# Context rows turned in 32x32 blocks and moved by way of DRAM in an attention kernel on one core, with the fourth block's period reordered

## The chip, the core and the metric

The kernel runs on one NeuronCore of a Trainium2 chip. The core's engines run side by side, each through its own list of instructions in order: TensorE (PE) multiplies matrices and loads weights (PEld), VectorE (DVE), ScalarE (ACT) and GpSimd (POOL) do elementwise work, reductions and 32x32 transposes, and SyncE (SP) issues most of the transfers. Engines wait for each other through semaphores. The metric is the time of one execution on the device in microseconds (us). A time below is the median of several runs.

## What is computed

Cross attention with adaptive layer norm, all in float32, for 16 batches of 1024 query rows and 64 context rows of 512 features, 16 heads of 32 features:

```python
def _ada_ln(x, c, W_ss, b_ss):
    h = (x - mean(x)) / sqrt(var(x) + EPS)
    scale, bias = split(silu(c) @ W_ss + b_ss, 2)
    return (1.0 + scale)[:, None, :] * h + bias[:, None, :]

xq  = _ada_ln(x_q,  t_vec, Wss_q,  bss_q)
xkv = _ada_ln(x_kv, t_vec, Wss_kv, bss_kv)
q    = xq @ Wq + bq
k, v = split(xkv @ Wkv + bkv, 2)              # per head
attn = softmax(q @ k.T / sqrt(32))            # per head
out  = x_q + (attn @ v) @ Wp + bp
```

The change concerns `xkv`: the normalised context rows have to be turned, features onto partitions, and get a scale and a bias for each feature and batch, before TensorE makes keys and values from them.

## The kernel before

The 16 x 1024 query rows are cut into 32 blocks of 512 rows, `i` = 0 to 31, two blocks to a batch. The schedule is written out by hand: a helper call issues its instructions at once onto the engines that it uses, so the order of calls is the order of each engine's queue. Blocks 0 to 3 have their periods written out line by line (the fourth block's period, `i` = 3, begins with `scores(3, 0)` at L1154 and ends with `q_scale(7)` at L1221). Blocks 4 to 29 run through one loop (L1224 to L1315), and a tail follows.

A period of the loop is a pipeline over several blocks. It makes the scores of block `i` in two halves (`scores`, L674: 32x32 matmuls into two pairs of PSUM banks of the pool `ps_s`, which has two buffers), their maxima (DVE, L698), a copy to SBUF (ACT, L707), the subtraction of the spread maxima (POOL, L742) and the exponential (ACT, L748). Beside this it mixes the values of block `a = i - 1` (`mix`, L839, L855), divides (`divided`, L835), and projects blocks `a` and `b = i - 2` as seven products each on half-size operands (`product`, L970, added to the residual by DVE at L994). It makes the queries of block `n = i + 1`, again as seven products (`query_product`, L633). Products 1, 6, 5 and 3 of the queries add up in one PSUM bank and 2, 7 and 4 in another; `query_added` (DVE, L670) reads the bank after product 5 and `query_out` (ACT, L663) after 2, 6, 7 and 3, and product 3 goes on in the bank that product 5 left, so it waits until `query_added(n, 5)` has read it.

Query rows of later blocks are prepared in the same periods: statistics (`q_stats`, DVE, L263 and L264; then `q_scale`), normalisation (`hidden`, ACT, L324), a 32x32 block transpose (`turn`, DVE, L503, into the tile `ht`), and sixteen transfers of 64 KB that carry the blocks to their partitions (`move`, L516, into `xt`). The pool of `ht` has **one buffer**. For blocks 1, 2, 3 and 5 half of the sixteen transfers are issued by POOL, all others by SP. `scale_features` (ACT, L573) and `feature_sums` (POOL, L608 to L611) then work on `xt`. The sums of the softmax (`row_total`, DVE, L791) are inverted and carried by way of a small DRAM tile (`inverse_rows`, L809 and L811: one store, four loads), and `spread_rows` (DVE, L817) spreads them.

Context rows come in pairs of batches: 128 rows, so one context tile serves four blocks. In the loop a pair `kvb` passes through four periods, by `kv = i % 4`: load and statistics (0); normalisation (`context_hidden`), four transposes on PE against an identity matrix into PSUM (`context_turned`, L351), scale on DVE (`context_scale`, L369) and shift on POOL (`context_shift`, L373) (1); keys (`key_products` on PE, L398, `key_tiles` on DVE, L409) (2); values (`value_products` on PE, L434, `value_tiles` on DVE, L447) (3). The PSUM results of these helpers lie in a `spare` buffer of `ps_s` (L345), the pool that the scores use. Pair 0 is made in the prologue. Pair 2 gets its features in the third block's period and its keys and values in the fourth (L1202, L1208, L1214, L1215).

Of the kernel before, what the change touches and what calls it, by code (L numbers as in the profile page):

```python
# [9 lines left out]
F32 = mybir.dt.float32  # L10
AF = mybir.ActivationFunctionType
ALU = mybir.AluOpType
# [3 lines left out]
P = 128  # L16
# [4 lines left out]
def cross_attention_block(  # L21
# [51 lines left out]
    nc = tc.nc  # L73

    B, LQ, H = x.shape
    LKV = context.shape[1]
# [69 lines left out]
    def load_residual(i):  # L146

        tag = "r" if i < NB - 1 else "x"
        r = xpool.tile([P, NT, H], F32, tag=tag, name=f"r_{i}")
        nc.sync.dma_start(r, rows_of(x, i))  # L150
        r_tiles[i] = r
# [13 lines left out]
    at = 0  # L165
# [133 lines left out]
    def q_stats(i, ts=range(NT), kvb=None):  # L299

        if ts[0] == 0:
            q_mv[i] = small.tile([P, NT + 1, 2], F32, tag="mvq", name=f"mvq_{i}")
        for t in ts:
            row_stats(q_mv[i][:, t, :], x_tiles[i][:, t, :])
        if kvb is not None:
            row_stats(q_mv[i][:, NT, :], ctx_tiles[kvb])
# [21 lines left out]
    def hidden(i, ts):  # L328

        for t in ts:  # L330
            normalise(x_tiles[i][:, t, :], x_tiles[i][:, t, :], q_rstd[i], t)
# [8 lines left out]
    def context_hidden(b):  # L340
        hk = kvpool.tile([P, H], F32, tag="hk", name=f"hk_{b}")
        normalise(hk, ctx_tiles.pop(b), *kv_rstd.pop(b))
        hk_tiles[b] = hk

    def spare(name):  # L345
        return ps_s.tile([P, 2, TB], F32, tag="s", name=name)[:, 0, :]

    def context_turned(b, pt):
        hk = hk_tiles.pop(b)
        for c in range(NC):  # L350
            nc.tensor.transpose(pt[:, c * P : (c + 1) * P], hk[:, c * P : (c + 1) * P], ident)  # L351
        xk_tiles[b] = kvpool.tile([P, NC, P], F32, tag="xk", name=f"xk_{b}")

    pkt_tiles = {}

    def context_scaled(b):
        pkt_tiles[b] = spare(f"pkt_{b}")
        context_turned(b, pkt_tiles[b])

    def by_batch(t):  # L360
        return t.rearrange("p c (j k) -> p c j k", j=2)

    def of_batches(b, at):
        t = ss["kv"][:, at : at + NC, b : b + 2]
        return t.unsqueeze(3).to_broadcast([P, NC, 2, LKV])

    def context_scale(b):
        pt = pkt_tiles.pop(b).rearrange("p (c k) -> p c k", c=NC)
        nc.vector.tensor_tensor(by_batch(xk_tiles[b]), by_batch(pt), of_batches(b, 0), ALU.mult)  # L369

    def context_shift(b):
        xk = by_batch(xk_tiles[b])
        nc.gpsimd.tensor_tensor(xk, xk, of_batches(b, NC), ALU.add)  # L373

    def context_features(b):
        pt = bank(f"pkt_{b}")
# [29 lines left out]
    def key_tiles(b):  # L406
        pk = pk_tiles.pop(b)
        kt = kvpool.tile([P, NC, P], F32, tag="kt", name=f"kt_{b}", bufs=2)
        nc.vector.tensor_tensor(  # L409
            kt,  # L410
            pk.rearrange("p (c k) -> p c k", c=NC),
            bk_t.unsqueeze(2).to_broadcast([P, NC, P]),
            ALU.add,
        )
        for j in range(2):
            k_tiles[b + j] = kt[:, :, j * LKV : (j + 1) * LKV]
# [153 lines left out]
    def scale_features(i, cs=range(NC)):  # L570
        xt, b = xt_tiles[i], i // BPB
        for c in cs:
            nc.scalar.activation(  # L573
                xt[:, :, c, :],
                xt[:, :, c, :],
                AF.Identity,
                scale=ss["q"][:, c, b : b + 1],
                bias=ss["q"][:, NC + c, b : b + 1],
            )
# [35 lines left out]
    def query_product(i, n):  # L615

        w, t = sums_of["wq"], sums_of["xt"]
        a, x = {
            1: (query_half(0, 0), feature_half(i, 0, 0)),
            2: (query_half(0, 1), feature_half(i, 1, 0)),  # L620
            3: (w[:, 3], feature_half(i, 1, 1)),
            4: (query_half(1, 1), t[:, 2]),
            5: (w[:, 0], feature_half(i, 0, 1)),
            6: (w[:, 1], t[:, 1]),
            7: (w[:, 2], t[:, 0]),
        }[n]
        k = 0 if n in (1, 6, 5, 3) else 1
        new = n in (1, 7)
        if new:
            qa[k] = bank(f"pq_{i}_{n}", k)  # L630
        for m in range(2):
            for c in range(HC):
                nc.tensor.matmul(  # L633
                    qa[k][:, m * HT : (m + 1) * HT].rearrange("p (g n) -> p g n", g=2),
                    lhsT=a[:, c, m * P : (m + 1) * P],
                    rhs=x[:, :, c, :],
                    start=new and m == 0 and c == 0,
                    stop=c == HC - 1,
                    skip_group_check=True,
                )  # L640
# [24 lines left out]
    def query_added(i, n):  # L665

        k, h = {5: (0, 1), 4: (1, 0)}[n]
        for o in (2, 3):
            src, dst = query_places(i, h, k, o)
            nc.vector.tensor_tensor(dst, src, dst, ALU.add)  # L670
# [118 lines left out]
    def row_total(i):  # L789
        lt_tiles[i] = small.tile([P, HPC, NJ], F32, tag="lt", name=f"lt_{i}")  # L790
        nc.vector.tensor_reduce(  # L791
            lt_tiles[i],
            sum_tiles.pop(i).rearrange("p r (j a) -> p r j a", a=32),
            AX.X,
            ALU.add,
            apply_transpose=True,
        )
# [393 lines left out]
    added(2, 1)  # L1191
    product(2, 2)
    added(2, 2)
    load_residual(3)
    q_stats(7)
    weights(3, 1)
    total(3)
    query_product(4, 7)
# [2 lines left out]
    row_sums(2, 1)  # L1201
    key_products(2, spare("pk_2"))  # L1202
    hidden(6, range(NT))
    query_product(4, 5)
    query_added(4, 5)
    row_total(3)
    inverse_rows(3)
    key_tiles(2)  # L1208
    query_product(4, 4)
    query_added(4, 4)  # L1210
    scale_features(5)
    turn(6, range(NT))
    load_x(8)
    value_products(2, spare("pv_2"))  # L1214
    value_tiles(2)  # L1215
    query_product(4, 3)
    query_out(4, 3)
    feature_sums(5)
    product(2, 7)
    move(6)  # L1220
    q_scale(7)  # L1221


    for i in range(4, NB - 2):  # L1224
        a, b, n, f = i - 1, i - 2, i + 1, i + 2
        kvb = i // 4 * 2 + 2
        kv = i % 4 if kvb < B else None
        if kv == 0:
            load_context(kvb)
        scores(i, 0, crossed=True)  # L1230
        product(b, 6)
        added(b, 6)
        query_product(n, 1)
        query_seed(n)
        added(b, 7)
        scores(i, 1)
        product(b, 5)
        added(b, 5)
        maxima(i)
        subtract(i)  # L1240
        product(b, 4)
        if i + 3 < NB:
            hidden(i + 3, (0, 1, 2))
        query_product(n, 2)
        query_out(n, 2)
        product(b, 3)
        spread_rows(a)
        if i + 3 < NB:
            hidden(i + 3, (3,))
        added(b, 4)  # L1250
        added(b, 3)
        biased(a, 2)
        load_residual(i)
        mix(a)
        divided(a)
        row_sums(a, 0)
        query_product(n, 6)
        weights(i, 0)
        query_out(n, 6)
        if kv == 1:  # L1260
            context_hidden(kvb)
        scale_features(f, (0, 1))
        product(a, 1)
        if i + 4 < NB:
            q_stats(i + 4, (0,))
        added(a, 1)
        product(a, 2)
        if i + 4 < NB:
            q_stats(i + 4, (1,))
        added(a, 2)  # L1270
        weights(i, 1)
        total(i)
        query_product(n, 7)
        query_out(n, 7)
        biased(a, 3)
        scale_features(f, (2, 3))
        row_sums(a, 1)
        if kv == 1:
            context_scaled(kvb)
        if kv == 2:  # L1280
            key_products(kvb, spare(f"pk_{kvb}"))
        if kv == 3:
            value_products(kvb, spare(f"pv_{kvb}"))
        if i + 3 < NB:
            turn(i + 3, range(NT))
        if i + 5 < NB:
            load_x(i + 5)
        elif i == NB - 3:
            load_residual(NB - 1)
        query_product(n, 5)  # L1290
        query_added(n, 5)
        if i + 4 < NB:
            q_stats(i + 4, (2,))
        if kv == 1:
            context_scale(kvb)
        if kv == 2:
            key_tiles(kvb)
        if kv == 3:
            value_tiles(kvb)
        query_product(n, 4)  # L1300
        query_added(n, 4)
        if i + 4 < NB:
            q_stats(i + 4, (3,), kvb=kvb if kv == 0 else None)
        query_product(n, 3)
        query_out(n, 3)
        feature_sums(f)
        product(a, 7)
        row_total(i)
        inverse_rows(i)
        if i + 3 < NB:  # L1310
            move(i + 3)
        if i + 4 < NB:
            q_scale(i + 4, kvb=kvb if kv == 0 else None)
        if kv == 1:
            context_shift(kvb)  # L1315

# [135 lines left out]
```

## Time and profile before

| What | Value |
|---|---|
| Median of 3 runs | 1044.82 us (1042.91 to 1045.44) |
| The profiled execution's own time | 1045.25 us |
| Its span, first to last instruction | 1043.3 us |
| DVE / ACT / POOL busy | 82% / 59% / 75% |
| Key products (L398), 256 matmuls in all | 29.9 us |
| Value products (L434), 1024 matmuls in all | 29.6 us |
| Context transposes on PE (L351), 32 matmuls | 4.8 us |
| Context scale on DVE (L369), 6 instructions | 3.9 us |
| Context shift on POOL (L373), 6 instructions | 6.3 us |

The page of a profile lists the busy time of the engines, the chain of work that ended last (followed back from the last instruction, each step to what released it), and groups of instructions with their time and the idle time ahead of them. The trace answers further questions: a timeline of one engine (start, length, line, shapes, and in brackets the idle time ahead with what ended it), sums by window, and landings of transfers. Matmuls overlap and their ends are modelled, so the time that a stretch of matmuls takes is read from start to start.

### The profile page before, as it was taken

The numbers are of one execution on the slowest core, as the hardware profiler recorded it, in microseconds if no ns is written. First come the engines' busy times: TensorE is split into PE (matmuls) and PEld (weight loads), VectorE is DVE, ScalarE is ACT, GpSimd is POOL, SyncE is SP. The second block draws the span as 40 slices with busy tenths as digits, with TensorE's granted clock in tenths as the row PEclk, the third lists the DMA queues.
The fourth block names the chain that finished last, engine by engine and source line by source line (L and its number), as shares of the span: only waits on it lengthen the run. The fifth ranks groups of instructions, "written<-read, shape, count | busy, mean of one in ns | idle before, by whom it ended". The sixth has DMA issues, their size and how long they took to land.

```text
span 1043.3 us, 22968 instructions
## 1 busy us (share of the span) xinstructions
PE 1021.9 (98%) x9058; PEld 760.0 (73%) x9058; DVE 854.4 (82%) x1159; ACT 610.9 (59%) x945; POOL 781.5 (75%) x502
## 2 busy tenths in 40 slices
PE   5999999999999999999999999999999999999998
PEld 3635686778777777777777787778787778777746
DVE  5798977987788977987878878898778997776795
ACT  3666755665567655766556666567557665565530
POOL 0479795887868868888668986688876886977861
PEclk9999999999999999999999999999999999999999
DMA  9851555444454434554335454344354444335122
GB/s 341 250 162 54 150 180 154 128 136 139 154 156 143 125 117 140 166 164 132 117 112 161 154 159 133 110 139 155 137 163 118 141 141 131 102 123 161 45 87 84
DMA packets 103499, 147.63 MB, mean 142 GB/s; under 512 B 33464, under 2 KB 34640, under 8 KB 103392
## 3 DMA queue, kind: packets, MB, share of 16 engines
q1 hardware_dynamic: 102368, 144.08, 43.5%
q0 software_dynamic: 1024, 2.10, 0.9%
q8 instruction: 71, 1.16, 0.5%
q14 instruction: 36, 0.29, 0.1%
HBM read 79.02 MB, written 34.60 MB: 109 GB/s over the span
## 4 chain that ended last, share of the span: by engine, by line
PE 91%; DVE 5%; DMA 1%; ACT 1%; POOL 1%; issue 1%; SPq 0%; DVEq 0%; ACTq 0%; POOLq 0%
PE pp L970 35%; PE pq L633 33%; PE po L855 6%; PE ps L681 6%; PE pq L546 4%; PE pv L434 3%; PE pk L398 3%; DVE m L698 1%; DMA x<-in_x_dram 1%; DVE bs L263 1%; DVE ht L503 0%; POOL s L742 0%; DVE lt L791 0%; ACT s L748 0%; DVE l L753 0%
## 5 line engine op out<-in xcount | busy, mean ns | idle before, releaser
L742 POOL TENSOR_TENSOR s<-s,mb 128x2048 f32<-128x2048 f32 x62 | 281.3, 4564 | 171.3 <-DVE mb L729 167.2
L707 ACT COPY s<-ps 128x1024 f32<-128x1024 f32 x128 | 129.4, 1012 | 112.7 <-DVE m L698 69.5
L698 DVE TRANSPOSE_TENSOR_REDUCE m<-ps 128x32 f32<-128x1024 f32 x128 | 150.8, 1215 | 31.1 <-PE ps L681 29.5
L970 PE MATMUL pp<-w_p_sb,ot 128*128 128x256 f32 x744 | 171.0, 379 | 0.9 <-DVE ot L835 0.5
L994 DVE TENSOR_TENSOR r<-pp,r 128x512 f32<-128x512 f32 x210 | 136.3, 670 | 32.1 <-PE pp L970 25.0
L663 ACT ACTIVATE qt<-pq,bias_t 128x256 f32<-128x256 f32 x224 | 92.6, 464 | 116.0 <-PE pq L633 113.3
L970 PEld LDWEIGHTS pp<-w_p_sb,ot 128*128 128x128 f32 x744 | 141.0, 190 | 21.8 <-issue 1.7
L748 ACT ACTIVATE s<-s 128x2048 f32<-128x2048 f32 x64 | 122.3, 1911 | 41.8 <-POOL s L742 40.0
L786 POOL TENSOR_TENSOR sum<-s,s 128x2048 f32<-128x2048 f32 x30 | 136.2, 4541 | 5.5 <-ACT s L748 5.5
L970 PEld LDWEIGHTS pp<-WT,s 128*128 128x128 f32 x496 | 90.6, 191 | 57.0 <-issue 35.2
L970 PE MATMUL pp<-WT,s 128*128 128x256 f32 x496 | 124.2, 394 | 0.2 <-POOL s L949 0.2
L970 PE MATMUL pp<-WT,ot 128*128 128x256 f32 x496 | 117.6, 380 | 1.0 <-POOL ot L946 0.6
L633 PE MATMUL pq<-xt_sums,wq_sums 128*128 128x256 f32 x448 | 108.5, 385 | 0.0
L633 PEld LDWEIGHTS pq<-xt_sums,wq_sums 128*128 128x128 f32 x448 | 82.9, 190 | 32.8 <-issue 21.8
L633 PE MATMUL pq<-xt,wq_sums 128*128 128x256 f32 x448 | 106.6, 381 | 0.0
L633 PE MATMUL pq<-xt,w_q_sb 128*128 128x256 f32 x448 | 106.0, 379 | 0.3 <-ACT pq L645 0.3
L970 PEld LDWEIGHTS pp<-WT,ot 128*128 128x128 f32 x496 | 93.9, 190 | 16.6 <-POOL ot L946 2.3
L324 ACT ACTIVATE x<-x,rstdq 128x512 f32<-128x512 f32 x128 | 96.6, 807 | 1.9 <-DVE rstdq L294 1.9
L670 DVE TENSOR_TENSOR qt<-pq,qt 128x256 f32<-128x256 f32 x112 | 42.0, 417 | 66.5 <-PE pq L633 66.1
L633 PEld LDWEIGHTS pq<-xt,w_q_sb 128*128 128x128 f32 x448 | 85.0, 190 | 13.1 <-ACT xt L573 0.8
L263 DVE BATCH_NORM_STATS2 bs<-x 128x6 f32<-128x512 f32 x128 | 86.9, 679 | 7.3 <-DMA x<-in_x_dram 7.3
L633 PEld LDWEIGHTS pq<-xt,wq_sums 128*128 128x128 f32 x448 | 83.5, 190 | 11.9 <-issue 1.4
(128 smaller groups left out, 1583.4 us busy)
## 6 DMA issues: line engine op xcount, KB each, us to landing
x<-in_x_dram SPq DMA_DIRECT2D x32, 1024.0 KB, 5.9
r<-in_x_dram SPq DMA_DIRECT2D x32, 1024.0 KB, 5.5
out_dram<-r SPq DMA_DIRECT2D x60, 512.0 KB, 3.7
xt<-ht SPq DMA_DIRECT2D x464, 64.0 KB, 2.0
wss_q<-in_L_xcond_Wss_q_dram SPq DMA_DIRECT2D x2, 1024.0 KB, 9.1
ctx<-in_ctx_dram SPq DMA_DIRECT2D x8, 256.0 KB, 3.1
wss_kv<-in_L_xcond_Wss_kv_dram SPq DMA_DIRECT2D x2, 1024.0 KB
w_kv_sb<-in_L_xcond_Wkv_dram SPq DMA_DIRECT2D x1, 2048.0 KB
```

What stands on the lines that cost most here:

```text
L263: nc.vector.bn_stats(bs, r)
L324: nc.scalar.activation(dst, src, AF.Identity, bias=rstd[:, 1, j : j + 1], scale=rstd[:, 0, j : j + 1])
L633: nc.tensor.matmul(qa[k][:, m * HT : (m + 1) * HT].rearrange("p (g n) -> p g n", g=2), lhsT=a[:, c, m * P : (m + 1) * P], rhs=x[:, :, c, : ...
L663: nc.scalar.activation(dst, src, AF.Identity, bias=bq_t[:, o : o + 1])
L681: nc.tensor.matmul(pss[r // 2][32 * c : 32 * c + 32, r % 2, :], lhsT=kt[rows, c, z * HK : (z + 1) * HK], rhs=qt[rows, c, :], start=True, s ...
L698: nc.vector.tensor_reduce(m_tiles[i][:, z, 2 * e : 2 * e + 2, :], pss[e].rearrange("p r (j a) -> p r j a", a=32), AX.X, ALU.max, apply_tra ...
L707: nc.scalar.copy(s_sb[:, 2 * e : 2 * e + 2, :], pss[e])
L742: eng.tensor_tensor(s_tiles[i, z], s_tiles[i, z], mb_tiles[i], ALU.subtract)
L748: nc.scalar.activation(p, p, AF.Exp, scale=SCALE)
L786: nc.gpsimd.tensor_tensor(t, s_tiles[i, 0], s_tiles[i, 1], ALU.add)
L970: nc.tensor.matmul(acc[k][:, t * HO : (t + 1) * HO], lhsT=rows[:, c, t * P : (t + 1) * P], rhs=cols[:, c, :], start=n == 2 and t == 0 and ...
L994: nc.vector.tensor_add(r, a, r)
```

## The change

The context rows no longer go over TensorE to be turned. `context_turn` transposes them on DVE in 32x32 blocks, `context_move` stores the result to a DRAM tile with one transfer and reads it back with four, and `context_moved` scales and shifts with eight ScalarE instructions of 128x64 elements. This holds for pairs 4 to 14; pairs 0 and 2 keep their way over PE. In the loop the turn and the move stand in the second of the four periods, the scaling in the third, the keys in the fourth, and the values in the first period of the blocks that use them (`i % 4 == 0`, pair `i // 2`). So pair 2's values leave the fourth block's period for the fifth's. The fourth block's period is reordered: `turn(6)` and `move(6)` go ahead of `key_tiles(2)`, `q_stats(7)` is spread out and ends in block 4's period together with `q_scale(7)`, `scale_features(5)` is cut in two, and `row_total(3)`, `inverse_rows(3)`, `load_x(8)` and `load_residual(3)` go behind `query_out(4, 3)`.

```diff
+    def context_turn(b):
+        t = kvpool.tile([P, 4, NC, 32], F32, tag="ctx", name=f"ctx_turned_{b}")
+        nc.vector.transpose(
+            t.rearrange("p k c n -> p c k n"),
+            hk_tiles.pop(b).rearrange("p (c k n) -> p c k n", c=NC, k=4),
+        )
+        turned_tiles[b] = t
+
+    def context_move(b):
+        d = dram.tile([4, 32, 4, NC * 32], F32, tag="ctx", name=f"ctxd_{b}")
+        m = kvpool.tile([P, 4, NC, 32], F32, tag="hk", name=f"ctx_moved_{b}")
+        nc.sync.dma_start(
+            d.rearrange("g f k n -> (g f) k n"),
+            turned_tiles.pop(b).rearrange("p k c n -> p k (c n)"),
+        )
+        for k in range(4):
+            nc.sync.dma_start(
+                m[32 * k : 32 * k + 32].rearrange("p g c n -> p g (c n)"),
+                d[:, :, k, :].rearrange("g f n -> f g n"),
+            )
+        moved_tiles[b] = m
+
+    def context_moved(b):
+        m, sk = moved_tiles.pop(b), ss["kv"]
+        xk_tiles[b] = kvpool.tile([P, NC, P], F32, tag="xk", name=f"xk_{b}")
+        for c in range(NC):
+            for j in range(2):
+                dst = xk_tiles[b][:, c, j * LKV : (j + 1) * LKV]
+                nc.scalar.activation(
+                    dst.rearrange("p (g n) -> p g n", g=2),
+                    m[:, 2 * j : 2 * j + 2, c, :],
+                    AF.Identity,
+                    scale=sk[:, c, b + j : b + j + 1],
+                    bias=sk[:, NC + c, b + j : b + j + 1],
+                )
...
@@ fourth block's period @@
-    load_residual(3)
-    q_stats(7)
     weights(3, 1)
     total(3)
     query_product(4, 7)
...
     key_products(2, spare("pk_2"))
     hidden(6, range(NT))
+    turn(6, range(NT))
+    move(6)
+    key_tiles(2)
     query_product(4, 5)
     query_added(4, 5)
+    q_stats(7, (0,))
+    query_product(4, 4)
+    query_added(4, 4)
+    q_stats(7, (1,))
+    scale_features(5, (0, 1))
+    query_product(4, 3)
+    query_out(4, 3)
+    scale_features(5, (2, 3))
     row_total(3)
     inverse_rows(3)
-    key_tiles(2)
-    query_product(4, 4)
-    query_added(4, 4)
-    scale_features(5)
-    turn(6, range(NT))
     load_x(8)
-    value_products(2, spare("pv_2"))
-    value_tiles(2)
-    query_product(4, 3)
-    query_out(4, 3)
+    load_residual(3)
     feature_sums(5)
     product(2, 7)
-    move(6)
-    q_scale(7)
...
@@ loop @@
         added(b, 7)
+        if i == 4:
+            q_stats(7, (2, 3))
+            q_scale(7)
         scores(i, 1)
...
-        if kv == 1:
-            context_scaled(kvb)
         if kv == 2:
+            context_moved(kvb)
+        if kv == 3:
             key_products(kvb, spare(f"pk_{kvb}"))
-        if kv == 3:
-            value_products(kvb, spare(f"pv_{kvb}"))
+        if i % 4 == 0:
+            value_products(i // 2, spare(f"pv_{i // 2}"))
...
         if kv == 1:
-            context_scale(kvb)
-        if kv == 2:
+            context_turn(kvb)
+        if kv == 3:
             key_tiles(kvb)
-        if kv == 3:
-            value_tiles(kvb)
+        if i % 4 == 0:
+            value_tiles(i // 2)
...
         if kv == 1:
-            context_shift(kvb)
+            context_move(kvb)
```

More of the change, by code (lines that the diff above doesn't have):

```diff
@@ L343, in context_hidden @@
         hk_tiles[b] = hk
+    turned_tiles, moved_tiles = {}, {}
+    def context_turn(b):
[31 more added lines that the diff above has]
+                )
     def spare(name):
@@ L352, in context_turned @@
         xk_tiles[b] = kvpool.tile([P, NC, P], F32, tag="xk", name=f"xk_{b}")
[L354 to L373, printed above, removed]
     def context_features(b):
```

## The prediction, made before the changed kernel ran

> **What bounds the kernel.** I read the page's busy times, then its chain of work that ended last, then the sums by period, then PE's timeline wherever PE stood still.
>
> ```profile
> PE 1021.9 (98%) x9058; PEld 760.0 (73%) x9058; DVE 854.4 (82%) x1159; ACT 610.9 (59%) x945; POOL 781.5 (75%) x502
> ...
> PE 91%; DVE 5%; DMA 1%; ACT 1%; POOL 1%; issue 1%; SPq 0%; DVEq 0%; ACTq 0%; POOLq 0%
> ```
>
> PE sets the end. The sums by window show it for the loop's four kinds of period (one period each, cut where `scores(i, 0)` starts; after the times: PE, PEld, DVE, ACT, POOL busy):
>
> ```profile
> 285.18:314.36 29.18, 29.18 (x241) 22.30 (x240) 26.18 (x37) 19.17 (x31) 20.75 (x13) 1.00 0.49 151
> 314.36:344.01 29.65, 29.65 (x246) 22.72 (x245) 26.64 (x36) 19.78 (x32) 24.88 (x16) 1.00 0.48 150
> 344.01:376.77 32.76, 32.76 (x274) 25.88 (x273) 26.25 (x36) 19.17 (x31) 28.41 (x19) 1.00 0.43 132
> 376.77:409.78 33.01, 33.01 (x369) 25.65 (x368) 26.24 (x37) 19.18 (x31) 24.58 (x17) 1.00 0.41 131
> ```
>
> PE is busy for all of each. The plain period takes 29.18 us; the transposes add 29.65 - 29.18 = 0.47, keys 3.58, values 3.83. In the loop only PE work that disappears can save time. PE stands still in the prologue, and one place of it lies in the reordered period (PE's timeline):
>
> ```profile
> 145.86 1.89 PE L633 MATMUL pq<-xt,wq_sums 128*128 128x256 f32 x8
> 147.59 1.89 PE L633 MATMUL pq<-xt_sums,w_q_sb 128*128 128x256 f32 x8
> 149.41 3.70 PE L434 MATMUL pv<-w_kv_sb,xk 128*32 128x128 f32 x128
> 153.04 1.99 PE L633 MATMUL pq<-xt,wq_sums 128*128 128x256 f32 x8
> 154.87 1.89 PE L970 MATMUL pp<-WT,ot 128*128 128x256 f32 x8
> 156.69 1.09 PE L681 MATMUL ps<-qt,kt 32*32 32x512 f32 x16
> 159.00 1.42 PE L681 MATMUL ps<-qt,kt 32*32 32x512 f32 x16 [1.22 <-DVE vt L447]
> 160.34 3.32 PE L970 MATMUL pp<-WT,s 128*128 128x256 f32 x8
> 163.50 1.89 PE L633 MATMUL pq<-xt,w_q_sb 128*128 128x256 f32 x8
> ```
>
> These are query products 5 and 4, pair 2's values, query product 3, `product(2, 7)`, then `scores(4, 0)`, whose second half waits for `value_tiles(2)` to free its PSUM buffer. Eight matmuls that go 1.73 us from start to start elsewhere then take 3.16; the windows say why (third number from the end: the granted clock):
>
> ```profile
> 157.00:160.30 3.30, 2.08 (x32) 0.21 (x16) 3.00 (x6) 0.00 (x0) 3.14 (x3) 0.90 0.25 47
> 160.30:163.50 3.20, 3.20 (x16) 2.57 (x9) 1.25 (x1) 1.93 (x2) 0.83 (x5) 0.57 1.04 353
> ```
>
> After the gap the clock was halved for some 3.4 us. In the loop the next query product starts 2.90 us after the scores do (219.41 to 222.31), here 163.50 - 156.69 = 6.81: the place loses **3.9 us**. Without loss, the scores would have had to start at 163.50 - 2.90 = 160.60; I call that their effective start.
>
> **Part 1, the transposes.** Six pairs lose four PE transposes each. Their durations mislead, because they overlap:
>
> ```profile
> 210.24 1.89 PE L633 MATMUL pq<-xt_sums,wq_sums 128*128 128x256 f32 x8
> 211.97 0.60 PE L351 MATMUL pkt<-ident,hk 128*128 128x128 f32 x4
> 212.40 1.89 PE L633 MATMUL pq<-xt,wq_sums 128*128 128x256 f32 x8
> ```
>
> Start to start the four take 0.43 us; the period is longer by 0.47 (above) or 0.44 (another, 29.63). 6 x 0.45 = **-2.7 us**. [...]
>
> **Part 2, what takes their place.** DVE: one 32x32 transpose of 128x512 (678 ns at L503) for one multiplication (657 ns at L369), in the same place: 0. POOL loses 1.05 us a pair: 0, it was not late. SP gets five transfers a pair behind `move`; SP's own waits show it idle 271.5 us over 32 periods ahead of `inverse_rows`, 8.5 each, against an estimated 5 us (issues of 0.4 us as at L811 and one wait for a store to land, where that wait at L811 is at most 4.4). Behind them stand output stores and `load_residual`, which is needed a period later. The reader, `context_moved`, comes some 15 us later: 0. ACT gets eight instructions of 128x64. The nearest row (L383: 16 in 4.9 us, so 0.31 each) gives 2.5 us. They stand ahead of `query_out(n, 3)`, before which ACT waited 2.33 us for PE in the plain period; that instruction comes 0.2 us late and then still ends 0.6 before the scores: 0. The layout in SBUF differs from the row's PSUM source; from half to twice the row, it costs nothing to 6 x 2 = 12 us. I take the row, as the operation and size are its own. [...]
>
> **Part 3, keys and values a period later.** The same PE work moves to other periods: 0. On DVE `value_tiles` (0.71) now shares a period with the context's statistics (0.84). That chain ends in the maxima and copies that `scores(i, 1)` needs, and the trace gives the margin. At 314.36 the first copy that frees a buffer ended at 318.31, 3.95 us after the scores' start; PE takes the buffer at 4.72. `query_added` waited 0.09 for PE, so 0.71 - 0.09 = 0.62 is handed down: 4.57, plus 0.06 from copy to PE as at 122.3. About 0.1 us is left: 0, but see rival B.
>
> **Part 4, the fourth block's period.** PE's list is now query products 5, 4, 3, `product(2, 7)`, scores. Without a wait, the scores start at 145.86 + 3 x 1.73 + 1.82 = 152.9. But `turn(6)` now stands on DVE ahead of `key_tiles(2)` and `query_added(4, 5)`, and writes `ht`, which has one buffer. The changed kernel's instruction order shows it waiting for all transfers of `move(5)`. Half of these are POOL's, and late, and the trace shows their landing through another reader:
>
> ```profile
> 143.10 4.00 POOL L516 DMA_DIRECT2D xt<-ht  x8
> ```
> ```profile
> 152.05 1.52 ACT L573 ACTIVATE xt<-xt,ss_q 128x512 f32<-128x512 f32 x2 [5.38 <-DMA xt<-ht]
> ```
>
> ACT could go on at 152.05; the last landing is recorded at 151.4, and a chain of waits follows. In the changed kernel the load of `r_3` no longer runs beside these transfers, so they may land up to 1.5 us sooner (150.0 is when the bytes ahead of that load are through). DVE starts the turn 0.9 after landing, at 150.9 to 152.3. Then turn 2.4, `key_tiles` 0.63, `query_added` 0.74 and 0.1 to PE: 3.9. Query product 3, which goes on in the bank that `query_added(4, 5)` reads, starts at 154.8 to 156.2 instead of 149.3. Six microseconds of idle PE, against 1.8 before, halve the clock again: the stretch recorded before lasted 3.4 us (1.7 lost); by where it falls, I bound the loss at 1.2 to 2.6 and take 2.0. PE then has 3.65 us left to the scores: 154.8 + 3.65 + 1.2 = 159.65 up to 156.2 + 3.65 + 2.6 = 162.45, middle **161.2**. The old loss goes, a new one of the same size comes.
>
> Behind the turn on DVE also wait `q_stats(7)`, `row_total(3)` and what SP does for it. SP issues 16 transfers at 0.63 from 154 on, so `inverse_rows(3)` lands near 169, before DVE reaches `spread_rows(3)` at 173; `load_x(8)` lands near 175 (needed 179), `load_residual(3)` near 178 (needed 180). In block 4's period DVE has 1.7 us more statistics against idle times of 1.0 and 0.4: 0 to 0.5 us.
>
> **Sum.** Scores 161.2 - 160.6 = +0.6; pair 2's values now follow, +3.83 (they lay ahead of the old start); transposes -2.7: **+1.7 us** (+0.2 to +3.0). The profiled execution took 1045.25 (span 1043.3 and 1.95 around it), 0.4 above the median; so 1046.5 to 1046.95, and I write 1046.8.
>
> **Rivals.** About 0.3%, 3.1 us, is what a measurement can tell from no change.
> - A, the turn does not hold DVE, as the transfers have landed by 146.7, when `hidden(6)` ends. Then `query_out(4, 3)`, behind `scale_features(5)` on ACT, sets the scores at 152.05 + 1.52 + 0.84 = 154.4: 161.2 - 154.4 = 6.8 us less, **1040.0**. For it: `r_3` is out of the way. Against: POOL issues its last transfer at 146.6. 0.10.
> - B, slower: the margin of 0.1 us before `scores(i, 1)` is gone. Place: the seven periods that follow one with values. Price: each 0.1 us that the copy comes later than I count, beyond the margin, is 0.7 us; from 0.2 us (1.4 in all) it decides, and at 0.5 it gives **1050.3**. For it: four small terms make that margin. Against: DVE's own idle times. The high price of ACT in part 2 goes with it. 0.22.
> - C, the clock is not halved, or the landing is early: scores at 159.2, **1044.8**, no change. 0.12.
> - The forecast: 0.56.
>
> Faster 0.10, same 0.56 + 0.12 = 0.68, slower 0.22. The range runs from below C, by the runs' own scatter of 1.3, to within B: 1043.5 to 1049.5.
>
> **What would show it.** Right: in the trace after, no L351 beyond pairs 0 and 2 and four kinds of period of 29.2, 29.2, 32.8 and 33.0 us in another order; DVE idle ahead of `turn(6)` until about 151.5 behind a DMA; PE idle some 6 us ahead of query product 3, then half clock. Wrong: PE without gap from 146 to 153 (A), PE waiting for an ACT copy once every four periods (B), or ACT's eight instructions far from 0.31 us.

## The result, and the profile after

The changed kernel takes **1048.7 us** (median of 4 runs, 1048.45 to 1049.06) against 1044.32 (4 runs, 1042.91 to 1045.44): ratio 1.0039, 95% interval 1.0022 to 1.0055. It is slower by 4.4 us, where 2.0 was forecast from the median. Its profiled execution took 1048.54 us, span 1046.7, 3.4 above the span before.

The page of the changed kernel, busy times and chain:

```profile
PE 1019.2 (97%) x9034; PEld 759.3 (73%) x9034; DVE 856.2 (82%) x1159; ACT 626.6 (60%) x993; POOL 775.0 (74%) x496
...
PE 88%; DVE 6%; DMA 2%; ACT 1%; issue 1%; POOL 1%; SPq 0%; DVEq 0%; ACTq 0%; POOLq 0%
```

PE has 24 matmuls and 2.7 us of work less (1021.9 to 1019.2), and yet the span is longer: PE's share of the chain fell from 91 to 88%, and VectorE's and the DMA's rose by one each. The line numbers behind L350 are higher by 19 now. The sums by window, one period each, cut as before (PE, PEld, DVE, ACT, POOL, then the granted clock):

```profile
195.23:224.41 29.18, 29.18 (x241) 22.33 (x240) 27.20 (x36) 20.15 (x34) 19.68 (x13) 1.00 0.44 138
224.41:253.60 29.19, 29.19 (x242) 22.36 (x241) 25.91 (x35) 21.52 (x38) 24.43 (x16) 1.00 0.45 141
253.60:286.50 32.90, 32.90 (x274) 26.04 (x273) 26.30 (x36) 19.41 (x32) 28.00 (x18) 1.00 0.48 161
286.50:319.51 33.01, 33.01 (x369) 25.69 (x368) 26.21 (x39) 18.90 (x29) 24.44 (x16) 1.00 0.44 139
```

The period of 29.65 is gone; PE is busy throughout, and the loop gained. Periods 5 to 29, from the start of `scores(5, 0)` to that of `scores(30, 0)`, took 776.86 us before and 774.77 now: -2.09.

PE's timeline in the fourth block's period:

```profile
146.87 1.89 PE L652 MATMUL pq<-xt_sums,w_q_sb 128*128 128x256 f32 x8
154.65 3.78 PE L652 MATMUL pq<-xt,wq_sums 128*128 128x256 f32 x8 [5.89 <-DVE qt L689]
158.23 2.06 PE L989 MATMUL pp<-WT,ot 128*128 128x256 f32 x8
160.22 1.14 PE L700 MATMUL ps<-qt,kt 32*32 32x512 f32 x32
```

Query product 3 waits 5.89 us for VectorE and then takes twice its time (3.78 us instead of 1.89). The windows show the granted clock (third number from the end) at 0.51 in the gap's second half and in what follows:

```profile
148.60:151.70 3.10, 0.16 (x1) 0.00 (x0) 0.83 (x2) 1.01 (x2) 3.10 (x2) 1.00 0.04 7
151.70:154.60 2.90, 0.00 (x0) 0.00 (x0) 2.90 (x7) 0.51 (x1) 1.68 (x2) 0.51 0.00 0
154.60:158.60 4.00, 3.95 (x9) 3.21 (x10) 3.93 (x7) 0.13 (x1) 0.00 (x0) 0.51 0.00 0
```

VectorE in the same place shows for whom it waited, in the step that the prediction named:

```profile
150.87 2.49 DVE L522 STREAM_TRANSPOSE ht<-x 128x512 f32<-128x512 f32 x4 [9.80 <-DMA xt<-ht]
...
153.86 0.74 DVE L689 TENSOR_TENSOR qt<-pq,qt 128x256 f32<-128x256 f32 x2
```

`turn(6)` stands still for 9.80 us until `move(5)` has landed, and `key_tiles(2)` and `query_added(4, 5)` (the last line) queue behind it.

The surprise lies one period later. PE's timeline in block 4's period:

```profile
173.11 2.35 PE L874 MATMUL po<-s,vt 32*32 32x512 f32 x64
175.39 1.99 PE L652 MATMUL pq<-xt_sums,wq_sums 128*128 128x256 f32 x8
179.14 3.04 PE L989 MATMUL pp<-w_p_sb,ot 128*128 128x256 f32 x13 [1.76 <-DVE ot L854]
```

The first product of block 3 (L989) waits for `divided(3)` on VectorE; from the start of the product before it, 3.75 us pass instead of 1.83. VectorE and SP show the chain behind that:

```profile
169.72 2.31 DVE L748 STREAM_TRANSPOSE mb<-m 128x2048 f32<-128x2048 f32 x1
174.38 2.31 DVE L836 STREAM_TRANSPOSE vb<-vr 128x2048 f32<-128x2048 f32 x1 [2.36 <-DMA vr<-ltd]
...
177.79 2.33 DVE L854 TENSOR_TENSOR ot<-po,vb 128x1024 f32<-128x1024 f32 x2
```
```profile
158.50 11.05 SPq L535 DMA_DIRECT2D xt<-ht  x16
169.66 0.52 SPq L828 DMA_DIRECT2D ltd<-lt  x1
171.33 1.75 SPq L830 DMA_DIRECT2D vr<-ltd  x4
```

`spread_rows(3)` (L836) waits 2.36 us for the inverted sums. These leave SP (L828) only behind the sixteen transfers of `move(6)`, and the first of these was issued at 158.50, though the turn had ended at 153.3. SP's waits in this stretch (140 to 180) name what held it; columns are total, times and longest:

```profile
SPq L535 <- PE pq L652: 5.0, 1, 5.0
```

`move(6)` writes `xt_6`, and the pool of `xt` (`qpool`) has two buffers. So `xt_6` takes the place of `xt_4`, which query product 3 of block 4 still reads; and that is the product which `turn(6)` had made late. The gap on PE is thus handed on: late turn, late product 3, late `move(6)`, late sums, late division.

### The profile page after: what moved, and what is told of

It is laid out like the page before. It is cut to its first block, busy times and chain, and to the rows that moved or that the text cites. A ratio compares the mean times of both kernels' runs of the same rounds, so it can differ in the third digit from the quotient of the medians.

```text
span 1046.7 us, 23002 instructions
## 1 busy us (share of the span) xinstructions
PE 1019.2 (97%) x9034; PEld 759.3 (73%) x9034; DVE 856.2 (82%) x1159; ACT 626.6 (60%) x993; POOL 775.0 (74%) x496
## 4 chain that ended last, share of the span: by engine, by line
PE 88%; DVE 6%; DMA 2%; ACT 1%; issue 1%; POOL 1%; SPq 0%; DVEq 0%; ACTq 0%; POOLq 0%
PE pp L989 34%; PE pq L652 32%; PE po L874 6%; PE ps L700 6%; PE pq L565 4%; PE pv L453 3%; PE pk L417 2%; DVE m L717 2%; DMA x<-in_x_dram 1%; DVE ht L522 1%; DVE bs L263 1%; DVE mb L748 0%; DVE vb L836 0%; POOL s L761 0%; DVE lt L810 0%
## 5 line engine op out<-in xcount | busy, mean ns | idle before, releaser
L989 PE MATMUL pp<-w_p_sb,ot 128*128 128x256 f32 x744 | 171.0, 380 | 2.7 <-DVE ot L854 2.3
L989 PEld LDWEIGHTS pp<-w_p_sb,ot 128*128 128x128 f32 x744 | 141.2, 190 | 23.7 <-ACT pp L952 2.1
L989 PEld LDWEIGHTS pp<-WT,s 128*128 128x128 f32 x496 | 89.9, 190 | 56.1 <-issue 30.7
L989 PE MATMUL pp<-WT,s 128*128 128x256 f32 x496 | 122.9, 391 | 0.2 <-POOL s L968 0.2
L989 PE MATMUL pp<-WT,ot 128*128 128x256 f32 x496 | 117.7, 381 | 1.0 <-POOL ot L965 0.6
L989 PEld LDWEIGHTS pp<-WT,ot 128*128 128x128 f32 x496 | 94.4, 191 | 16.6 <-POOL ot L965 2.3
```

The source lines that it names most:

```text
L989: nc.tensor.matmul(acc[k][:, t * HO : (t + 1) * HO], lhsT=rows[:, c, t * P : (t + 1) * P], rhs=cols[:, c, :], start=n == 2 and t == 0 and ...
```

## The experiments

Theory P: the added time comes from the place of `turn(6)` and `move(6)` in the fourth block's period (the gap of PE with its half clock, and the wait for the division). Rivals: L, the loop with its new route of the context rows costs time; V, only pair 2's values (3.83 us), which went from under an old wait to a period that had none; D, VectorE's own work in its new order, whatever the transfers do. In each edit below, "-" and "+" are against the changed kernel, unless another is named. Ratios are to the kernel before, run on the same chip, with a 95% interval. The experiments ran on three chips, on which the kernel before took 1043.8 to 1045.0 us, so differences to the changed kernel's 1048.7 are between chips.

**e1, the turn and the move back.**

```diff
-    turn(6, range(NT))
-    move(6)
     key_tiles(2)
...
+    turn(6, range(NT))
     scale_features(5, (0, 1))
...
     product(2, 7)
+    move(6)
```

> The changed kernel, but turn(6) and move(6) stand where they stood before the change (the turn behind query_added(4, 4), the move at the period's end). Theory P (place): in the changed kernel turn(6), which waits for the transfers of block 5, holds VectorE and through it query product 3 (6.05 us of idle PE and 1.9 us of half clock, against 3.9 us lost before the change), and move(6) ahead of inverse_rows(3) on SP makes product(3, 1) wait another 2.0 us. Then the scores of block 4 start some 7 us sooner (ScalarE's query_out behind scale_features(5) is next, about 1 us late), the 2.0 us go, and 0.5 to 1.5 us come at scores(4, 1), since row_total(3) now ends late: 1048.7 - 7 - 2 + 1 = 1040.7 us. Rival L (loop): the trip through DRAM, ScalarE's scaling and the moved keys and values cost in every cycle of four blocks; the gap in the fourth block's period only takes the place of the old one: about 1048. Rival V (values): pair 2's values, 3.83 us, added to block 4's period, are the loss, and without the turn's wait the old loss of 3.9 us returns there: about 1045.

Measured: 1042.33 us (12 runs; before 1045.04), ratio 0.9981 (0.9969 to 0.9993). The clock is not halved (0.999 or 1.000 in all twelve). PE's timeline of e1:

```profile
150.86 1.89 PE L989 MATMUL pp<-WT,ot 128*128 128x256 f32 x8
153.24 1.51 PE L700 MATMUL ps<-qt,kt 32*32 32x512 f32 x32 [0.50 <-ACT qt L682]
```

The product ahead of the scores starts at 150.86 instead of 158.23, the scores at 153.24 instead of 160.22. Two helper calls put back turn +4.4 us into -2.7 by medians (-2.0 by the ratio). It is 1.6 us above what was expected; small losses stay in the trace, 0.9 us before these scores (a query sum on ScalarE), 0.65 before their second half and 0.5 before block 3's first product.

**e2, the loop alone**: the fourth block's period as before the change (its whole text and the values in it), the loop as after.

```diff
@@ the fourth block's period is not shown again @@
...
-        if i % 4 == 0:
+        if i > 4 and i % 4 == 0:
             value_products(i // 2, spare(f"pv_{i // 2}"))
...
```

> The loop's part of the change alone: pairs 4 to 14 turned on VectorE, moved by way of DRAM, scaled on ScalarE, their keys and values in the new periods; the fourth block's period as before the change, pair 2's values in it. Theory P: PE loses 24 transposes of 0.11 us and nothing waits anew: 1044.3 - 2.1 (as the sum over periods 5 to 29 of the two profiles) = 1042.2 us, and the scores of block 4 start as before the change. Rival L: not below 1044.3. Rival V: 1042.2.

Measured: 1042.77 us (12 runs), 0.9977 (0.9966 to 0.9988). Periods 5 to 29 take 774.67 us, as in the changed kernel (774.77). Rival L falls: the loop's part gains.

**e3, the period alone**: the fourth block's period as after, the loop as before; in period 4 only, pair 2's values and the rest of `q_stats(7)`.

```diff
@@ against the kernel before; the period's new order is not shown again @@
...
+        if i == 4:
+            value_products(2, spare("pv_2"))
...
+        if i == 4:
+            value_tiles(2)
```

> The fourth block's period alone: its new order, with pair 2's values and the rest of q_stats(7) in block 4's period; pairs 4 to 14 go over PE as before the change. Theory P: before + 10.0 us lost at the new places - 3.9 us lost at the old = 1044.3 + 6.1 = 1050.4 us. Rival L: 1044 to 1045. Rival V: 1048.2 (the 3.83 us of the values alone).

Measured: 1050.73 us (6 runs), 1.0068 (1.0052 to 1.0083). PE's timeline of e3 shows the same wait and the same stretched product (its lines keep the numbers of before):

```profile
154.96 3.78 PE L633 MATMUL pq<-xt,wq_sums 128*128 128x256 f32 x8 [6.04 <-DVE qt L670]
```

By medians the parts give -2.3 and +5.7, together +3.4, and the change as a whole +4.4; by the ratios they give -2.4 and +7.1, together +4.7, and the whole +4.1. The period carries the loss, the loop the gain.

**e4, the move behind the sums**: the turn stays early, the sixteen transfers go behind `inverse_rows(3)`.

```diff
     turn(6, range(NT))
-    move(6)
...
     inverse_rows(3)
+    move(6)
     load_x(8)
```

> The changed kernel, but move(6) is issued behind inverse_rows(3); turn(6) stays. Theory P: SP no longer waits for query product 3 and 16 issues before the row sums go out, they land some 8 us sooner, spread_rows(3) waits for nothing, and product(3, 1) starts 2.0 us sooner; the gap before query product 3 stays at 6 us and the half clock with it: 1048.7 - 2.0 = 1046.7 us. Rivals L and V: 1048.7, no change.

Measured: 1047.34 us (12 runs), 1.0028 (1.0018 to 1.0038), 1.4 below the changed kernel's 1048.7. PE's timeline, then SP's, of e4:

```profile
155.28 3.78 PE L652 MATMUL pq<-xt,wq_sums 128*128 128x256 f32 x8 [5.96 <-DVE qt L689]
...
176.50 1.99 PE L652 MATMUL pq<-xt_sums,wq_sums 128*128 128x256 f32 x8
178.33 3.62 PE L989 MATMUL pp<-w_p_sb,ot 128*128 128x256 f32 x16
```
```profile
160.30 0.35 SPq L828 DMA_DIRECT2D ltd<-lt  x1
...
164.21 10.90 SPq L535 DMA_DIRECT2D xt<-ht  x16
```

The gap is unchanged, but block 3's first product follows without a wait: the sums leave at 160.30 instead of 169.66. Block 4's period takes 33.09 us instead of 35.01. This shows the second loss by itself, 1.92 us, and that its cause was SP's queue. The span fell by only 0.9, because the fourth period's scores started 1.03 later (0.56 of that already stood ahead of the reordered lines).

**e5, a tile of its own** for block 5's turned rows, so that `turn(6)` writes to another buffer.

```diff
-            pool, tag = (big, "big2") if i == 2 else (hpool, "ht")
+            pool, tag = (big, "big2") if i == 2 else (big, "big1") if i == 5 else (hpool, "ht")
```

> The changed kernel with every call in its place; only block 5's turned rows lie in a tile of their own (the place of a score tile that is free then), so turn(6) no longer waits for the transfers that read them. Theory P: VectorE does the turn while it had stood idle, some 144 to 147 us, query product 3 waits about 1 us or less, no half clock; ScalarE's query_out(4, 3) behind scale_features(5) then sets the scores, about 1 us late. move(6) still stands ahead of inverse_rows(3) and still waits for query product 3, so the 2.0 us before product(3, 1) stay: 1048.7 - 7 = 1041.7 us. Rival D (VectorE's work): the turn itself, 2.4 us in front of query_added, is what costs, wherever its input comes from: 1046 or more.

Measured: 1040.33 us (5 runs; before 1043.79), 0.9968 (0.9956 to 0.9981). All of the order stays as in the changed kernel; only the buffer differs. PE's and SP's timelines of e5:

```profile
148.48 1.89 PE L652 MATMUL pq<-xt,wq_sums 128*128 128x256 f32 x8
```
```profile
150.44 10.81 SPq L535 DMA_DIRECT2D xt<-ht  x16
161.35 0.52 SPq L828 DMA_DIRECT2D ltd<-lt  x1
```

With product 3 on time (the product after it starts at 150.21), `move(6)` is issued at 150.44, right behind it: the wait for `xt` again. The gap, the half clock (0.999 or 1.000 now in all five) and half of the second loss go with one name of a tile; 0.91 us are left before block 3's first product. Rival D falls: VectorE does the same turn in the same place.

**e7, the values back in the gap**: pair 2's values between query products 4 and 3, as they stood before.

```diff
+    value_products(2, spare("pv_2"))
+    value_tiles(2)
     query_product(4, 3)
...
-        if i % 4 == 0:
+        if i > 4 and i % 4 == 0:
             value_products(i // 2, spare(f"pv_{i // 2}"))
```

> The changed kernel, with pair 2's values back in the fourth block's period, between query products 4 and 3, where PE stands idle. Theory P: the 3.6 us of values run inside the wait and cost nothing there, the start of the scores moves by 0 to 2 us (less idle time, perhaps less half clock), and block 4's period is 3.8 us shorter; the 2.0 us before product(3, 1) stay: 1048.7 - 3.8 to 5.8 = 1043 to 1045 us. Rival D: the same work in front of the scores delays them, 1048.7.

Measured: 1044.17 us (11 runs), 1.0000 (0.9991 to 1.0009). PE's timeline of e7:

```profile
149.15 3.70 PE L453 MATMUL pv<-w_kv_sb,xk 128*32 128x128 f32 x128
154.90 2.95 PE L652 MATMUL pq<-xt,wq_sums 128*128 128x256 f32 x8 [2.05 <-DVE qt L689]
```

The wait for `turn(6)` is still there, shorter by some 3.8 us, and the scores start at 160.24 as against 160.22: here the values cost nothing. The loss before block 3's first product was expected to stay at 2.0 us and is 0.8 (the product starts 2.66 us after the one before it, instead of 1.83). Rival V is right about the price, wrong about the rest: e1 keeps the values where the change put them, and is 6.4 us faster than the changed kernel.

**e8, three mends at once**: e5's tile; `move(6)` behind `inverse_rows(3)`; and `query_out(4, 3)` ahead of all of `scale_features(5)` on ScalarE.

```diff
@@ e5's line is not shown again @@
     turn(6, range(NT))
-    move(6)
     key_tiles(2)
...
-    scale_features(5, (0, 1))
     query_product(4, 3)
     query_out(4, 3)
-    scale_features(5, (2, 3))
+    scale_features(5)
     row_total(3)
     inverse_rows(3)
+    move(6)
     load_x(8)
     load_residual(3)
```

> A version that should beat both: the changed kernel with the tile of its own for block 5's turned rows, move(6) behind inverse_rows(3), and query_out(4, 3) ahead of scale_features(5) on ScalarE. Theory P: PE runs without a wait from the keys of pair 2 through block 4's period, or with 0.5 us lost; against the changed kernel 8.0 + 2.0 us go, to 1038.5 to 1039.5 us (about 5.5 below the kernel before: its 3.9 us and the loop's 2.1). Rival D: 1044 or more.

Measured: 1041.73 us (11 runs), 0.9975 (0.9964 to 0.9986): a miss. The reordered places are clean (scores at 152.44, as soon as the product ahead of them is through), but a new wait arose in block 4's period, where block 5's queries are made. PE, VectorE and SP of e8:

```profile
180.26 1.89 PE L652 MATMUL pq<-xt_sums,w_q_sb 128*128 128x256 f32 x8
185.07 2.59 PE L652 MATMUL pq<-xt,wq_sums 128*128 128x256 f32 x8 [2.92 <-DVE qt L689]
```
```profile
176.24 0.69 DVE L263 BATCH_NORM_STATS2 bs<-x 128x6 f32<-128x512 f32 x1 [5.80 <-DMA x<-in_x_dram]
...
179.90 0.69 DVE L1013 TENSOR_TENSOR r<-pp,r 128x512 f32<-128x512 f32 x1 [2.75 <-DMA r<-in_x_dram]
```
```profile
158.96 10.04 SPq L535 DMA_DIRECT2D xt<-ht  x16
169.09 0.53 SPq L143 DMA_DIRECT2D x<-in_x_dram  x1
169.66 0.54 SPq L150 DMA_DIRECT2D r<-in_x_dram  x1
```

The sixteen transfers now stood ahead of two loads, and VectorE waited for both. In the profiled execution PE lost some 3.1 us by waiting and 1.8 by a stretch of half clock (0.60 from 187.00 to 190.40): 4.9 in all. That execution is the highest of the eleven (1043.42); in nine of them, the median among these, the granted clock was 1.000, so the 1041.73 holds no half clock.

**e10, the move last**: e8 with `move(6)` at the period's end, behind both loads.

```diff
@@ against e8 @@
     inverse_rows(3)
-    move(6)
     load_x(8)
     load_residual(3)
     feature_sums(5)
     product(2, 7)
+    move(6)
```

> As e8_all_three (own tile for context block 5's turned rows, the query sum of product 3 ahead of the scaling of block 5's features), but move(6) stands at the end of block 4's period, behind load_x(8) and load_residual(3). In e8_all_three these two loads were issued at 169.09 and 169.66, behind sixteen transfers of move(6) that took SP from 158.96 on; VectorE then waited 5.80 for x and 2.75 for r, and TensorE lost 4.9 us before query product 3 of block 5 (2.92 of waiting and a stretch at half clock). Theory P (each loss in blocks 3 to 5 is a queue behind move(6) or the turned rows' buffer): the loads leave at about 157 and 158, VectorE has both by 169, the 4.9 us are gone, nothing new takes their place: 1041.7 - 4.9 = 1036.8 us, and no half clock after 142. Rival Q (the wait in block 5 comes from VectorE's own order, added(3,1) ahead of turn(7), whatever SP does): 1041 to 1042, with query product 3 of block 5 again at about 185. Rival R (move(6) at the end lands too late for feature_sums(6) and the query products of block 6): 1038 to 1040, with a DMA wait in block 5's second half.

Measured: 1039.33 us (5 runs; before 1044.87), **0.9946** (0.9931 to 0.996): the fastest of all, faster than both kernels. It missed its 1036.8: 2.4 us came back by medians (2.6 between the profiled executions), not 4.9. The 4.9 had been read from e8's profiled execution with its half clock and taken from a median without one; and new waits arose. VectorE did not wait for the two loads and the half clock is gone (0.999 or 1.000 in all five), so rival Q (VectorE's own order) falls. Rival R gave the number and the mechanism, a `move(6)` that lands too late, though it looked for the loss a period later. PE, ScalarE and VectorE of e10:

```profile
179.04 1.99 PE L652 MATMUL pq<-xt,wq_sums 128*128 128x256 f32 x8
181.89 1.97 PE L652 MATMUL pq<-xt_sums,w_q_sb 128*128 128x256 f32 x8 [0.85 <-ACT qt L682]
```
```profile
177.70 1.52 ACT L592 ACTIVATE xt<-xt,ss_q 128x512 f32<-128x512 f32 x2 [4.96 <-DMA xt<-ht]
...
180.93 0.81 ACT L682 ACTIVATE qt<-pq,bias_t 128x256 f32<-128x256 f32 x2
```
```profile
177.72 2.49 DVE L522 STREAM_TRANSPOSE ht<-x 128x512 f32<-128x512 f32 x4 [3.23 <-DMA xt<-ht]
```

ScalarE waits 4.96 us for `move(6)`'s transfers before it can scale block 6's features, and `query_out(5, 7)` behind that (at 180.93) is what query product 4 of block 5 waits for: PE loses 1.1 us there, plus 0.3, 0.3 and 0.5 in three spots earlier. `turn(7)` waits 3.23 us for the same transfers to free `ht`, the wait that the change gave to `turn(6)`, one block later and shorter; it does not hold PE here, as VectorE then waits for ScalarE another 1.20 us.

**e11, e1 with the query sum first**, to see whether turning block 6 early is worth anything.

```diff
@@ against e1 @@
-    scale_features(5, (0, 1))
     query_product(4, 3)
     query_out(4, 3)
-    scale_features(5, (2, 3))
+    scale_features(5)
```

> As e1_turn_back (the turn and the move of block 6 where they stood before the change), and the query sum of product 3 ahead of all of scale_features(5) on ScalarE. In e1_turn_back ScalarE waited 4.83 us for DMA at 151.31 inside scale_features(5), with the query sum behind it, and scores(4,0) lost about 0.9 us. Theory P: only that loss goes: 1042.3 - 0.9 = 1041.4 us, scores(4,0) within 0.1 us of the end of the product before it; the 0.65 before the second scores and the 0.52 before product(3,1) stay, so e10_move_last must be 3 us or more faster than this one. Rival S (turning block 6 early gives nothing by itself, the own tile and the order on SP do all): this one comes within 1 us of e10_move_last.

Measured: 1040.7 us (7 runs), 0.9965 (0.9953 to 0.9977). The scores start at 152.16 without a wait, as expected, and the median fell from 1042.33 to 1040.7. But the other losses did not stay as they were: in the profiled execution (1042.83; the seven lie at 1040.3 to 1040.7 and at 1042.3 to 1043.1) PE lost 1.6 us before the second half of the scores, where 0.65 was expected, and 1.9 before query product 4 of block 5, behind ScalarE's wait for `move(6)`. No trace shows one of the shorter executions. The 3 us that e10 was to be ahead are 1.4, and the ratios' intervals overlap: whether the early turn by itself gains is not settled.

**e9, the scaling twice**: ScalarE scales and shifts each context tile two times (the same values are written again), to test the cover of its 2.75 us a pair.

```diff
-        for c in range(NC):
+        for c in tuple(range(NC)) * 2:
```

> The changed kernel, with every context scaling on ScalarE done twice (the second pass writes the same values), 2.75 us more for each of six pairs. Theory P says that the first pass costs nothing because ScalarE would have waited 2.3 us for PE ahead of query_out(n, 3), with some 0.6 us more before the scores need that result; a second pass has no cover: about 2.75 + 2.75 - 2.3 - 0.6 = 2.6 us for each pair, 15 us in all, 1064 us. Rival L' (ScalarE has room enough anywhere): 1048.7.

Measured: 1062.05 us (4 runs), 1.0173 (1.0159 to 1.0187), 13.4 us above the changed kernel, 2.2 a pair. Three of the four executions show a lower granted clock (0.994 to 0.995) than the profiled one (0.997), so a part of the 13.4 is half clock; in the profiled one periods 5 to 29 took 787.41 us instead of 774.77, 2.1 a pair. ScalarE's and PE's timelines of e9, and the group of instructions in the changed kernel (busy time, mean ns of one):

```profile
248.83 5.41 ACT L377 ACTIVATE xk<-ctx_moved,ss_kv 128x64 f32<-128x64 f32 x16
254.14 0.82 ACT L682 ACTIVATE qt<-pq,bias_t 128x256 f32<-128x256 f32 x2
```
```profile
254.65 1.51 PE L700 MATMUL ps<-qt,kt 32*32 32x512 f32 x32 [1.70 <-ACT qt L682]
```
```profile
L377 ACT ACTIVATE xk<-ctx_moved,ss_kv 128x64 f32<-128x64 f32 x48 | 16.5, 431 | 0.0
```

One pass is hidden, a second shows at 2.1 of its 2.7 us. In the changed kernel these 16.5 us cost nothing that the windows show (the period with them takes 29.19, the plain one 29.18).

## Why the prediction was right in kind and short in size

- **PE bounds the kernel, and the transposes are gone**: right. The loop gained 2.09 us where 2.7 was worked out (2.19 in e2). The missing 0.6 is in single spots: the start of the query product behind the mix (L874) is 0.10 to 0.15 us late in six periods (0.74 in sum), before in two (0.17). What makes these spots is open.
- **ScalarE's eight instructions cost nothing**: right. They took 0.344 us each, not 0.31; e9 shows that their cover is real and ends within the second pass. The halving or doubling of their price that the prediction allowed did not occur.
- **Keys and values a period later**: right, and rival B with it is refuted. The second half of the scores starts 4.72 us after the first in the period that follows one with values (195.23 to 199.95), as PE alone would have it, and so it does in every other period of the loop.
- **`turn(6)` waits for `move(5)`'s landing**: right, and the largest wait. VectorE started at 150.87 (150.9 to 152.3 was given), product 3 at 154.65 (154.8 to 156.2), the half clock took 1.92 us (2.0). Two terms in this were the author's estimates: the 0.9 us from landing to start, where the trace before shows 0.65 at ScalarE (151.4 to 152.05), and the bounds of 1.2 and 2.6 around the half clock's loss, which no run shows. The profiled execution was 0.72 ahead already at pair 2's key products (142.29 before, 141.57 now). The change alters no call up to there, and the lead is scatter of the start: the first key products, which stand in the prologue, begin at 36.04 before and at 35.30 now, over all twelve profiled executions at 35.06 to 36.04, and from there to pair 2's keys each of the twelve takes 106.25 to 106.28 us. Counted from there, the scores came 0.34 later than the effective start before; +0.6 was worked out.
- **Pair 2's values, +3.83**: right.
- **The step that failed**: "SP issues 16 transfers at 0.63 from 154 on, so `inverse_rows(3)` lands near 169", and with it "0 to 0.5 us" for block 4's period. The transfers began at 158.50, not 154, and took 0.69 each, and the sums landed near 174.3, 5 us after the forecast 169. The prediction looked at the single buffer that `turn(6)` writes, and not at the two of the tile that `move(6)` writes. Its reader is the query product that had just been made late, so the late start was in the prediction's own numbers: with product 3 at 154.8 to 156.2 and half clock, `xt_4` could not be free before 158. PE lost 2.0 us; e4 took away just this, and block 4's period shrank by 1.92.
- **The range**: 1048.7 lies within 1043.5 to 1049.5, but not by the sum's own bounds: +3.0 us on the 1044.8 that it started from is 1047.8. The room above that was left for rival B, which did not come. What filled it was the missed wait, so that the range held is luck in this respect.

In spans: start -0.72, fourth period +0.34, values +3.83, the missed wait +2.0, the loop -2.09, tail +0.1: +3.46 against 3.4 observed. In medians it is 4.4, because the profiled execution before was 0.9 above its median and the one after 0.2 below. The 0.9 has a cause on record: that execution holds the stretch of half clock (0.998 over its span), and not every execution of the kernel before does (last section).

What stays open: the late spots behind the mix, why the prologue varies by up to 1 us, and whether turning early gains by itself.

## What to carry to other kernels

When a step is pulled forward, check the buffer that it writes **and** the buffer that every later step of its chain writes: here the turn waited 9.80 us for the old reader of `ht` and the move 5.0 us for that of `xt`, and what stood behind them on VectorE and SP waited too. Sixteen transfers took SP 11.05 us in the changed kernel, 10.04 in e8 and 16.11 in e10, a wall for all that stands behind them, so what is needed soonest (here four small loads of sums, then two of rows) goes ahead of it. When work is taken out of a gap, the gap can stay (PE waited 5.89 us here without the values and 2.05 with them, in e7): it must be shown that what made the gap is gone as well.

## What the runs showed of the hardware

The record of the granted clock holds one stretch of half clock around the reordered place in each of the two kernels. Before, it lasts 3.41 us, from 159.64 to 163.06 (0.50, and 1.00 in the 3.41 us on either side); in the changed kernel it lasts 6.83 us, from 151.73 to 158.56 (0.50, and 1.00 on either side). The kernel before does not show it in every execution. It was run 62 times beside the experiments. In 26 of these the granted clock over the span was 0.999 or more (median 1043.1 us), in 36 it was 0.998 or less (1045.4 us), as one stretch of 3.41 us at half speed makes it over the span of 1043.3. What decides between the two was not shown, as only one execution of each kernel was traced. The changed kernel had 0.996 or 0.997 in all four, so against the kernel before with its half clock it loses some 3.3 us.

Four waits of PE come with half clock: 1.22 us before (up to 159.00), 5.89 in the changed kernel (up to 154.65), 2.05 in e7 (up to 154.90) and 2.92 in e8 (up to 185.07). In e7 the granted clock was 0.63 from 154.90 to 158.30, in e8 0.60 from 187.00 to 190.40. From the product behind the wait to the scores, 5.34 us pass in both, against 3.55 in e10 (183.69 to 187.24), so the two waits each cost 1.8 us more than they last. The wait of 1.76 us in the changed kernel (up to 179.14) and that of 0.85 us in e10 (up to 181.89) passed at 1.00, and so did a stretch of e11 in which PE was busy for 1.98 of 3.50 us (155.00 to 158.50). So the length of the wait alone does not settle it, as 1.22 us came with half clock and 1.76 us did not; what does is not shown by these runs.
